# One load moved in the DMA queue, and the first two graphs' work put in another order, in a two-layer graph kernel

## The chip, the cores and the metric

The kernel runs on one core of a Trainium2 chip. A core has five engines that work side by side: TensorE (PE in the profile; PEld is its loading of weights), VectorE (DVE), ScalarE (ACT), GpSimd (POOL) and SyncE (SP), which here issues nearly all DMA transfers. The metric is the device time of one execution in microseconds (us); lower is better. Three runs of the kernel before took 2946.97 to 2951.11 us, with a median of 2949.02.

## The reference

64 graphs of N = 256 nodes with F = 512 features go through two layers; each adds its outcome to its input and normalises the rows. Layer 0 is a graph attention with 8 heads of 64 features: the logits are a sum of two numbers per node, and only neighbours are seen. Layer 1 is ordinary attention with the adjacency added to its weights.

```python
# layer 0
feats = einsum('bnf,hfu->bhnu', X, W)
e_self, e_neigh = feats . a_self, feats . a_neigh
att = softmax(leaky_relu(e_self[i] + e_neigh[j], 0.2) where A else -1e10)
x = layernorm(x + relu(att @ feats + b))
# layer 1
q, k, v = split(x @ W_qkv)
attn = softmax(q @ k.T / 8 where mask) * 0.33
attn = attn + 0.33 * adj + 0.33 * exp(-adj)          # both only where mask
x = layernorm(x + (attn @ v) @ W_out + b_out)
```

All numbers are 32-bit floats.

## The kernel before, in words

**Tiling.** A graph's 256 nodes are two tiles (T = 2) of 128 rows, its 512 features four chunks (C = 4) of 128. The four large products of a graph (features `pf`, queries and keys `pq`, values `pv`, output `po`) are each done with seven block products instead of eight (`seven`, `seven_rows`; steps "p1" to "p7"). For this, sums and differences of blocks are needed: of the activations (`left_factors`, giving `xC`, `hC`, `oC`) and, once, of the weights (`right_factors`, `combine_weights1`, giving parts of `wf_sb`, `wqk_sb`, `wv_sb`, `wo_sb`). PE multiplies and writes to PSUM; ACT copies the running sum of a chain of products to SBUF (L320), DVE adds the products that stand alone (L323).

**The order of the work** is written out by hand: `do(stage, b, step)` records the instructions of one step of graph b, and `in_order()` ties them to that order on each engine. So an engine runs its instructions in the order of the source, and one that waits holds up all behind it. Three routines follow one another:

- `start()` does layer 0 of graphs 0 and 1 and the q and k products of layer 1 of graph 0. Graph 0's and 1's features are plain products (`features`, L595) which DVE takes from PSUM (`copied`, L618, adding the bias). `maxima` transposes the logits to rows (`pr`), takes their maxima (L530) and broadcasts them with a small product (`pn`, L536); `columns` (L559, `nd`) and `factors` make the factors of the attention weights per column and per row, the latter spread over the partitions by products with a selection matrix (`pg`, L548) and kept in PSUM. `weights` multiplies them on DVE (`pT`, L669), `product` multiplies with the features on PE (`av`, L692). `shared` (L466 to L481) prepares the part of layer 1's weights that all heads share, `attention_vectors` (`pw`, `pwa`, L418) folds the attention vectors into the feature weights.
- A loop over b from 1 to 63 calls `attention0_beside_projections1(b)` and `attention1_beside_projections0(b)`. One turn holds work of four graphs: layer 1's attention of graph b−2 and b−1, layer 0's attention of b, its features of b+1. A turn of the trace is counted here from its first `pz` product (layer 1's scores).
- `end()` finishes the last graphs.

**The DMA queue.** SP issues the transfers of a turn in the order of the source. Around the change that is: `gs`, `gb` (row factors to DRAM and back, spread over the partitions), `rs`, `rb` (layer 1's inverse row sums, the same way, 1 MB), then `load_rows(b + 1)` (L138: x's rows, 0.5 MB, which `end` at L735 adds to layer 0's outcome), and in the next call `store` (`out_dram<-y`, L1113, 0.5 MB) and `rows_again` (`y<-hs`, L989, 0.5 MB: layer 0's outcome read back from DRAM). `rows_again` takes the buffer that `store` reads, so SP waits for that store to land before it issues it. `load_rows` takes the buffer of tag "hb".

Of the kernel before, what the change touches and what calls it, by code (L numbers as in the profile page):

```python
# [8 lines left out]
FT = mybir.dt.float32  # L9
# [8 lines left out]
def kernel(  # L18
# [56 lines left out]
    def ps_tile(shape, name):  # L75

        return psum.tile(shape, FT, tag="mm", name=name, bufs=4)

    matmul = nc.tensor.matmul
# [56 lines left out]
    def load_rows(b):  # L136
        X[b] = io.tile([P, T, F], FT, tag="hb", name=f"x_{b}", bufs=1)
        nc.sync.dma_start(X[b], x[b].rearrange("(t p) f -> p t f", p=P))  # L138
# [102 lines left out]
    def load_weights1():  # L241

        wk1 = work.tile([P, C2, F], FT, tag="p", name="wk1", bufs=5)
        wv12 = work.tile([P, C2, F2], FT, tag="both", name="wv12", bufs=4)
        parts = w_qkv.rearrange("(k c p) (h s u) -> s k c p h u", k=2, p=P, s=3, u=U)

        def get(dst, s, k, heads=slice(0, H)):
            for c in range(C2):
                nc.sync.dma_start(
                    dst[:, c].rearrange("p (h u) -> p h u", u=U), parts[s, k, c][:, heads]  # L250
                )

        get(wqk_sb[:, 0], 0, 0)
        get(wqk_sb[:, 1], 0, 1)
        get(wk1, 1, 0)
        get(wqk_sb[:, 6], 1, 1)
        get(wv_sb[:, 0], 2, 0, slice(0, HG))
        get(wv12, 2, 0, slice(HG, H))
        get(wv_sb[:, 1], 2, 1, slice(0, HG))
        get(wv_sb[:, 2], 2, 1, slice(HG, H))  # L260

        def combine(part):
            q1, q2, s1, s2, s3, s4, k2 = (wqk_sb[:, i] for i in range(7))
            if part == 0:
                nc.vector.tensor_add(s1, wk1, k2)
                nc.vector.tensor_sub(s2, s1, q1)
            elif part == 1:
                nc.vector.tensor_sub(s3, q1, wk1)
            elif part == 2:
                nc.vector.tensor_sub(s4, q2, s2)  # L270
            else:
                right_factors(wv_sb, wv12)
            in_order()

        return combine
# [163 lines left out]
    def proj0(b):  # L439
# [12 lines left out]
        FAR = {}  # L452
# [7 lines left out]
            nc.scalar.copy(mrow, MROW[b])  # L460
            FAR[1] = mrow

        def shared():
            mrow = FAR[1]
            CT[b] = work.tile([P, T, N], FT, tag="ct", name=f"ct_{b}", bufs=3)
            nc.vector.tensor_add(CT[b], pa, FAR[0])  # L466
            for j in range(T):
                nc.vector.scalar_tensor_tensor(
                    CT[b][:, j, :],
                    CT[b][:, j, :],  # L470
                    m33[:, j, b : b + 1],
                    mrow,
                    op0=ALU.mult,
                    op1=ALU.mult,
                )
# [43 lines left out]

        ROW = {}  # L520

        def maxima():

            ps = ps_tile([H, 2, N], f"pr_{b}")
            for s in range(2):
                for t in range(T):
                    transpose(ps[:, s, t * P : (t + 1) * P], V0[b][:, t, :, U + s])
            grow = small.tile([H, N + 1], FT, tag="grow", name=f"grow_{b}", bufs=1)
            nb = small.tile([H, 1], FT, tag="nb", name=f"nb_{b}", bufs=2)
            nc.vector.tensor_reduce(grow[:, N : N + 1], ps[:, 1, :], AX.X, ALU.max)  # L530
            nc.vector.tensor_scalar_mul(nb, grow[:, N : N + 1], -0.8)
            nc.scalar.activation(grow[:, :N], ps[:, 0, :], AF.Exp, bias=nb, scale=-0.8)
            diag = small.tile([H, H], FT, tag="diag", name=f"diag_{b}", bufs=1)
            nc.vector.tensor_scalar_mul(diag, ident[:H, :H], grow[:, N : N + 1])
            ROW["max"] = ps_tile([P, H], f"pn_{b}")
            matmul(ROW["max"], sel[:, H, :], diag, start=True, stop=True)  # L536
            ROW["rows"] = grow

        def factors():
            grow = ROW["rows"]  # L540
            nc.vector.tensor_scalar(
                grow[:, :N], grow[:, :N], 1.0, TINY, op0=ALU.min, op1=ALU.max
            )
            GB[b] = []
            for g in range(2):
                pg = psum.tile([P, HG, N], FT, tag="sc", name=f"pg_{b}_{g}", bufs=2)
                for k in range(HG):
                    matmul(  # L548
                        pg[:, k, :],
                        sel[:, g * HG + k, :],  # L550
                        grow[:, :N],
                        start=True,
                        stop=True,
                    )
                    GB[b].append(pg[:, k, :])

        def columns():
            nd = small.tile([P, T, H], FT, tag="nd", name=f"nd_{b}", bufs=2)
# [578 lines left out]
    def do(stage, b, step, *args):  # L1137

        if 0 <= b < NB:
            if (stage, b) not in S:  # L1140
                S[stage, b] = stages[stage](b)
            S[stage, b][step](*args)
            in_order()

    def start():
# [18 lines left out]
        attention_vectors(1, 0)  # L1164
        do("proj0", 0, "maxima")
        attention_vectors(0, 1)
        do("turned", 1, "xT")
        load(2)
        do("proj0", 0, "columns")
        do("proj0", 0, "factors")  # L1170
        for h in range(H):
            do("proj0", 0, "scaled", h)
            do("attend0", 0, "weights", h)
# [15 lines left out]
        attention_vectors(3, 1)  # L1189
        attention_vectors(2, 2)  # L1190
        attention_vectors(3, 2)
        combine_weights1(0)
        for t in range(T):
            for g in range(2):
                do("proj0", 1, "features", t, g)
        do("attend0", 0, "norm", tiles[0])
        do("proj0", 0, "shared")
        do("proj0", 1, "aT")
        load_rows(1)
        do("turned", 2, "xT")  # L1200
        right_factors(wf_sb, wf12)
        in_order()
        for t in range(T):
            for g in range(2):
                do("proj0", 1, "copied", t, g)
        do("proj0", 1, "maxima")
        do("proj0", 1, "columns")
        do("proj1", 0, "from_rows", 0)
        do("attend0", 0, "norm", tiles[1])
        do("proj1", 0, "qk", "p1")  # L1210
        do("proj1", 0, "from_rows", 1)
        do("proj1", 0, "blocks")
        do("proj1", 0, "hC")
        do("proj1", 0, "qk", "p2")
        do("proj0", 1, "far")
        do("proj0", 1, "factors")
        combine_weights1(1)
        combine_weights1(2)
        load_adj(2)
        do("proj1", 0, "qk_add", 11)  # L1220
        do("proj1", 0, "qk", "p6")
        for h in range(HG):
            do("proj0", 1, "scaled", h)
            do("attend0", 1, "weights", h)
        do("proj1", 0, "qk", "p5")
        do("proj1", 0, "qk", "p7")
        do("proj1", 0, "qk_add", 22)
        combine_weights1(3)
        for h in range(HG, H):
            do("proj0", 1, "scaled", h)  # L1230
            do("attend0", 1, "weights", h)
        do("proj1", 0, "qk", "p4")
        do("proj1", 0, "qk", "p3")
        do("proj1", 0, "qk_add", 12)
        do("turned", 2, "xC")

    def attention0_beside_projections1(b):


        if b > 1:  # L1240
            do("attend1", b - 4, "squares")
            do("proj1", b - 1, "qk", "p1")
            do("proj1", b - 1, "qk", "p2")
            do("proj0", b, "columns")
            do("attend1", b - 4, "store")
            do("attend1", b - 3, "rows_again")
            do("proj1", b - 1, "qk", "p6")
            for h in range(HG):
                do("proj0", b, "scaled", h)
                do("attend0", b, "weights", h)  # L1250
            do("proj1", b - 1, "qk_add", 11)
            for h in range(HG, H):
                do("proj0", b, "scaled", h)
            do("proj1", b - 1, "qk", "p5")
            for h in range(HG, H):
                do("attend0", b, "weights", h)
            do("proj1", b - 1, "qk", "p7")
            do("proj1", b - 1, "qk_add", 22)
            if b + 1 < NB:
                do("turned", b + 1, "xC")  # L1260
# [60 lines left out]
    def attention1_beside_projections0(b):  # L1321
# [32 lines left out]
        do("attend1", b - 2, "product", "p4")  # L1354
        do("proj0", b + 1, "bias")
        do("softmax1", b - 1, "inverted")
        if b + 1 < NB:
            load_rows(b + 1)
        do("attend1", b - 2, "product", "p3")
        do("attend1", b - 2, "product_add", 12)  # L1360
        if b == 1:
# [129 lines left out]
```

## Time and profile before

| | |
|---|---|
| runs, median (lowest to highest) | 2949.02 us (2946.97 to 2951.11) |
| profiled execution, its own time | 2945.5 us |
| its span, first to last instruction | 2943.7 us |
| PE busy | 2893.2 us, 98% |
| DVE busy | 2595.7 us, 88% |
| ACT busy | 1784.6 us, 61% |
| DMA, mean over the span | 123 GB/s |

The profile is one execution taken by the hardware profiler. "L12" is a line of the kernel. A row of the page's groups gives an engine's line and operation, output and input, the count, the busy time and the mean of one, and the engine's idle time just before with what ended it. The chain that ended last is followed back from the last instruction through whatever released each step; "issue" in it is time in which an engine waited for nothing that the profile shows. A row of the windows gives the stretch, then the busy time of PE, PEld, DVE, ACT and POOL in it, each with its count of instructions, and at its end the granted share of PE's clock, the busy share of the DMA engines and GB/s. The trace also holds a record of each DMA packet with its queue, start and size. Idle time of an engine that isn't the bottleneck costs nothing.

### The profile page before, as it was taken

To read this page: it belongs to the slowest core of one execution; us is meant where nothing else is said; L and a number is where in the kernel's file an instruction comes from. 1 tells how busy PE (TensorE), PEld (TensorE's weight loads), DVE (VectorE), ACT (ScalarE), POOL (GpSimd) and SP (SyncE) were. 2 spreads that over 40 slices of the span, in tenths; PEclk is the share of its full clock that TensorE was granted. 3 is DMA by queue.
4 is the path that set the end of the run, shared out by engine and by line. 5 is a ranking of instruction groups with operands and counts; after the bars stand their busy time and mean duration, and the time that the engine had idled before them with its cause. 6 is when DMAs were issued, how large, how long until landed. Compare 5 with 4: busy or idle time off the path is not lost.

```text
span 2943.7 us, 67840 instructions
## 1 busy us (share of the span) xinstructions
PE 2893.2 (98%) x26302; PEld 2475.2 (84%) x26302; DVE 2595.7 (88%) x5147; ACT 1784.6 (61%) x4905; POOL 210.1 (7%) x526
## 2 busy tenths in 40 slices
PE   8999999999999999999999999999999999999998
PEld 6788888888888888888888888888888888888886
DVE  5788989999989989999989989899998989989984
ACT  2556665666666666566666656666666666666563
POOL 0000000000000000000000000000000000000001
PEclk8999999999999999999999999999999999999999
DMA  6444454454454454454444554544544554545432
GB/s 127 94 125 117 128 137 109 131 136 116 127 138 109 130 130 122 128 127 125 130 120 124 138 117 127 136 108 130 140 110 127 135 119 129 124 120 139 117 109 69
DMA packets 778871, 362.23 MB, mean 123 GB/s; under 512 B 694604, under 2 KB 696636, under 8 KB 762552
## 3 DMA queue, kind: packets, MB, share of 16 engines
q1 hardware_dynamic: 776440, 357.37, 48.4%
q8 instruction: 210, 3.44, 0.5%
q14 instruction: 109, 0.89, 0.1%
q10 hardware_dynamic: 2112, 0.52, 0.1%
HBM read 289.42 MB, written 68.13 MB: 121 GB/s over the span
## 4 chain that ended last, share of the span: by engine, by line
PE 95%; DVE 2%; issue 1%; DMA 1%; ACT 1%; SPq 0%; POOL 0%; DVEq 0%; POOLq 0%; ACTq 0%
PE pq_p L311 27%; PE pf_p L311 13%; PE pv_p L311 13%; PE po_p L311 13%; PE av L692 9%; PE pz L859 8%; PE av L975 7%; PE pd L893 2%; PE pr L82 1%; PE po L1096 0%; PE pg L548 0%; SPq L114 0%; DMA gb<-gs 0%; DMA x<-in_x_dram 0%; ACT junk L363 0%
## 5 line engine op out<-in xcount | busy, mean ns | idle before, releaser
L311 PE MATMUL pq_p<-hC,wqk_sb 128*128 128x128 f32 x4096 | 495.2, 279 | 6.9 <-ACT qk L320 3.2
L311 PEld LDWEIGHTS pq_p<-hC,wqk_sb 128*128 128x128 f32 x4096 | 470.0, 193 | 24.4 <-ACT qk L320 17.3
L669 DVE SCALAR_TENSOR_TENSOR pT<-gb,ccol,at 128x256 f32<-128x256 f32 x992 | 403.1, 477 | 55.1 <-ACT ccol L566 55.1
L311 PE MATMUL pq_p<-hT,wqk_sb 128*128 128x128 f32 x3072 | 366.9, 276 | 2.0 <-DVE hT L121 1.4
L311 PEld LDWEIGHTS pq_p<-hT,wqk_sb 128*128 128x128 f32 x3072 | 360.9, 193 | 6.2 <-DVE hT L121 1.8
L873 ACT ACTIVATE p<-pz,hide 128x512 f32<-128x512 f32 x512 | 316.9, 686 | 76.5 <-PE pz L859 39.1
L965 DVE TENSOR_TENSOR p<-p,ct 128x1024 f32<-128x1024 f32 x252 | 308.7, 1225 | 8.6
L723 ACT ACTIVATE x<-av,rec 128x64 f32<-128x64 f32 x1008 | 221.0, 336 | 151.4 <-DVE rec L705 151.4
L958 DVE TENSOR_TENSOR p<-p,rb 128x1024 f32<-128x1024 f32 x252 | 304.1, 1207 | 4.9 <-DMA rb<-rs 4.9
L692 PE MATMUL av<-v,pT 128*64 128x65 f32 x8192 | 259.0, 224 | 13.7 <-issue 12.6
L692 PEld LDWEIGHTS av<-v,pT 128*64 128x64 f32 x8192 | 247.9, 139 | 24.1 <-issue 16.4
L859 PE MATMUL pz<-qk 64*128 64x256 f32 x2048 | 256.2, 389 | 0.9 <-ACT p L873 0.9
L626 ACT ACTIVATE v<-v 128x64 f32<-128x64 f32 x1024 | 251.8, 339 | 0.0
L311 PE MATMUL pf_p<-wf_sb,xC 128*128 128x264 f32 x992 | 251.2, 386 | 0.0
L311 PE MATMUL pv_p<-wv_sb,hC 128*128 128x256 f32 x1024 | 242.9, 380 | 4.1 <-ACT v L320 4.1
L859 PEld LDWEIGHTS pz<-qk 64*128 64x128 f32 x2048 | 187.1, 186 | 65.5 <-issue 46.0
L311 PE MATMUL po_p<-wo_sb,oC 128*128 128x256 f32 x992 | 234.5, 379 | 0.5 <-ACT o L320 0.5
L320 ACT COPY v<-pv_p 128x256 f32<-128x256 f32 x256 | 95.6, 373 | 225.8 <-PE pv_p L311 225.7
L975 PE MATMUL av<-p,v 128*64 128x256 f32 x2016 | 231.9, 382 | 0.2 <-DVE p L965 0.2
L311 PEld LDWEIGHTS pv_p<-wv_sb,hC 128*128 128x128 f32 x1024 | 194.9, 191 | 32.6 <-ACT v L320 4.9
L311 PEld LDWEIGHTS pf_p<-wf_sb,xC 128*128 128x128 f32 x992 | 187.8, 190 | 31.5 <-ACT v L320 0.3
L311 PEld LDWEIGHTS po_p<-wo_sb,oC 128*128 128x128 f32 x992 | 187.8, 190 | 27.2 <-ACT o L320 0.9
(163 smaller groups left out, 4442.1 us busy)
## 6 DMA issues: line engine op xcount, KB each, us to landing
rb<-rs SPq DMA_DIRECT2D x63, 1024.0 KB
gb<-gs SPq DMA_DIRECT2D x62, 1028.0 KB
hs<-x SPq DMA_DIRECT2D x64, 512.0 KB
xb<-in_x_dram SPq DMA_DIRECT2D x252, 128.0 KB
x<-in_x_dram SPq DMA_DIRECT2D x63, 512.0 KB
hb<-hs SPq DMA_DIRECT2D x252, 128.0 KB
y<-hs SPq DMA_DIRECT2D x63, 512.0 KB
out_dram<-y SPq DMA_DIRECT2D x63, 512.0 KB
```

What stands on the lines that cost most here:

```text
L311: matmul(d, lhsT, rhs, start=(p in FIRST and i == 0), stop=(i == len(todo) - 1), skip_group_check=True,)
L320: nc.scalar.copy(out[COPIES[p]], dst)
L626: nc.scalar.activation(V0[b][:, t, h, :U], V0[b][:, t, h, :U], AF.Copy, scale=V0[b][:, t, h, U : U + 1],)
L669: nc.vector.scalar_tensor_tensor(pT[h][:, j, :], GB[b][h], CCOL[b][:, j, h : h + 1], AT[b][:, j, :], op0=ALU.max, op1=ALU.mult,)
L692: matmul(av[r * half : (r + 1) * half, k, :], pT[h][:, j, i : i + half], V0[b][:, j, h, :UA], start=(j == 0), stop=(j == T - 1),)
L723: nc.scalar.activation(X1[b][:, t, h * U : (h + 1) * U], av[:, k, :U], AF.Copy, scale=REC0[g][:, t, k : k + 1],)
L859: matmul(pz[:, r, j, :], QK[b][rows, g, 1, j * P : (j + 1) * P], QK[b][rows, g, 0, :], start=True, stop=True,)
L873: nc.scalar.activation(p[:, :, j, :], pz[:, :, j, :], AF.Exp, bias=hide[:, j, b : b + 1], scale=U**-0.5,)
L893: matmul(pd[k * 32 : (k + 1) * 32, g // 2, :], ones, both[g][:, r, :], start=True, stop=True, tile_position=(0, 32 * k),)
L958: nc.vector.tensor_mul(p, p, REC[b][:, k : k + 2, g // 2, :] .unsqueeze(2) .to_broadcast([P, 2, T, N]),)
L965: nc.vector.tensor_add(p, p, CT[b].unsqueeze(1).to_broadcast([P, 2, T, N]))
L975: matmul(av[0][r * U : (r + 1) * U, g % 2, :], V1[b][:, j, 2 * g + r, :], PROBS[b][g][:, r, j, :], start=(j == 0), stop=(j == T - 1),)
```

## The change

In the loop, `load_rows` goes from the end of one call to the middle of the next: behind `rows_again` instead of behind `rb`. In `start()`, the order is changed and three steps are split: `combine_weights1(0)` in two halves (0 and 4), `shared` in two (0: the first addition; 1: the rest), `maxima` in two (the small product `pn` alone as part 1). For graph 0, `pn`, `columns` and `factors` come ahead of graph 1's transposes, and the first four heads' factors go to two PSUM tiles of two heads instead of one of four. For graph 1, its four feature products are copied by DVE one by one with other work between them; q's and k's first products of graph 0 follow behind them, and the transposes of graph 2 and the feature weights' `right_factors` go to the routine's end. No computation is added or left out, and PE, DVE, ACT and SP have the same instructions as before.

```diff
@@ combine(part)
             if part == 0:
                 nc.vector.tensor_add(s1, wk1, k2)
+            elif part == 4:
                 nc.vector.tensor_sub(s2, s1, q1)
@@ shared
-        def shared():
+        def shared(part=None):
             mrow = FAR[1]
-            CT[b] = work.tile([P, T, N], FT, tag="ct", name=f"ct_{b}", bufs=3)
-            nc.vector.tensor_add(CT[b], pa, FAR[0])
+            if part != 1:
+                CT[b] = work.tile([P, T, N], FT, tag="ct", name=f"ct_{b}", bufs=3)
+                nc.vector.tensor_add(CT[b], pa, FAR[0])
+            if part == 0:
+                return
@@ maxima
-        def maxima():
+        def maxima(part=None):
+            if part == 1:
+                ROW["max"] = ps_tile([P, H], f"pn_{b}")
+                matmul(ROW["max"], sel[:, H, :], ROW["diag"], start=True, stop=True)
+                return
...
-            ROW["max"] = ps_tile([P, H], f"pn_{b}")
-            matmul(ROW["max"], sel[:, H, :], diag, start=True, stop=True)
-            ROW["rows"] = grow
+            ROW.update(rows=grow, diag=diag)
@@ factors
-            for g in range(2):
-                pg = psum.tile([P, HG, N], FT, tag="sc", name=f"pg_{b}_{g}", bufs=2)
-                for k in range(HG):
...
+            h = 0
+            while h < H:
+                n = 2 if b == 0 and h < HG else HG
+                if n == 2:
+                    pg = ps_tile([P, n, N], f"pg_{b}_{h}")
+                else:
+                    pg = psum.tile([P, n, N], FT, tag="sc", name=f"pg_{b}_{h}", bufs=2)
+                for k in range(n):
+                    matmul(pg[:, k, :], sel[:, h + k, :], grow[:, :N], start=True, stop=True)
                     GB[b].append(pg[:, k, :])
+                h += n
@@ start
         attention_vectors(0, 1)
+        do("proj0", 0, "maxima", 1)
+        do("proj0", 0, "columns")
+        do("proj0", 0, "factors")
         do("turned", 1, "xT")
         load(2)
-        do("proj0", 0, "columns")
-        do("proj0", 0, "factors")
@@ start, behind attention_vectors(3, 2)
-        combine_weights1(0)
         for t in range(T):
             for g in range(2):
                 do("proj0", 1, "features", t, g)
         do("attend0", 0, "norm", tiles[0])
-        do("proj0", 0, "shared")
+        do("attend0", 0, "norm", tiles[1])
+        do("proj0", 1, "copied", 0, 0)
+        combine_weights1(0)
+        do("proj0", 1, "copied", 0, 1)
+        combine_weights1(4)
+        do("proj0", 1, "copied", 1, 0)
+        do("proj0", 0, "shared", 0)
         do("proj0", 1, "aT")
-        load_rows(1)
-        do("turned", 2, "xT")
-        right_factors(wf_sb, wf12)
-        in_order()
-        for t in range(T):
-            for g in range(2):
-                do("proj0", 1, "copied", t, g)
-        do("proj0", 1, "maxima")
-        do("proj0", 1, "columns")
+        do("proj0", 1, "copied", 1, 1)
         do("proj1", 0, "from_rows", 0)
-        do("attend0", 0, "norm", tiles[1])
-        do("proj1", 0, "qk", "p1")
         do("proj1", 0, "from_rows", 1)
         do("proj1", 0, "blocks")
+        load_rows(1)
+        do("proj0", 1, "maxima")
+        do("proj1", 0, "qk", "p1")
+        do("proj0", 1, "maxima", 1)
+        do("proj0", 1, "columns")
+        do("proj1", 0, "qk", "p2")
         do("proj1", 0, "hC")
-        do("proj1", 0, "qk", "p2")
+        do("proj0", 1, "factors")
+        do("proj0", 0, "shared", 1)
         do("proj0", 1, "far")
-        do("proj0", 1, "factors")
-        combine_weights1(1)
-        combine_weights1(2)
         load_adj(2)
         do("proj1", 0, "qk_add", 11)
+        combine_weights1(1)
         do("proj1", 0, "qk", "p6")
         for h in range(HG):
             do("proj0", 1, "scaled", h)
             do("attend0", 1, "weights", h)
+        combine_weights1(2)
         do("proj1", 0, "qk", "p5")
         do("proj1", 0, "qk", "p7")
-        do("proj1", 0, "qk_add", 22)
-        combine_weights1(3)
         for h in range(HG, H):
             do("proj0", 1, "scaled", h)
+        do("proj1", 0, "qk_add", 22)
+        for h in range(HG, H):
             do("attend0", 1, "weights", h)
         do("proj1", 0, "qk", "p4")
         do("proj1", 0, "qk", "p3")
         do("proj1", 0, "qk_add", 12)
+        combine_weights1(3)
+        do("turned", 2, "xT")
         do("turned", 2, "xC")
+        right_factors(wf_sb, wf12)
+        in_order()
@@ attention0_beside_projections1(b), b > 1
             do("attend1", b - 4, "store")
             do("attend1", b - 3, "rows_again")
+            load_rows(b)
@@ attention1_beside_projections0(b)
         do("softmax1", b - 1, "inverted")
-        if b + 1 < NB:
-            load_rows(b + 1)
```

More of the change, by code (lines that the diff above doesn't have):

```diff
@@ L544, in factors @@
             GB[b] = []
-            for g in range(2):
-                pg = psum.tile([P, HG, N], FT, tag="sc", name=f"pg_{b}_{g}", bufs=2)
-                for k in range(HG):
[L548 to L554, printed above, removed]
+            h = 0
[7 more added lines that the diff above has]
+                    matmul(pg[:, k, :], sel[:, h + k, :], grow[:, :N], start=True, stop=True)
                     GB[b].append(pg[:, k, :])
+                h += n
         def columns():
```

## The prediction

> **What bounds the kernel now.** I read the busy table and the chain that ended last first: TensorE (PE) carries 95% of it, so only time in which PE stands still or runs at half clock can be won or lost.
>
> ```profile
> PE 2893.2 (98%) x26302; PEld 2475.2 (84%) x26302; DVE 2595.7 (88%) x5147; ACT 1784.6 (61%) x4905; POOL 210.1 (7%) x526
> PE 95%; DVE 2%; issue 1%; DMA 1%; ACT 1%; SPq 0%; POOL 0%; DVEq 0%; POOLq 0%; ACTq 0%
> ```
>
> Then the same chain in order of time, two turns of the loop (columns: start, us, what):
>
> ```profile
> 828.74 5.62 PE pq_p L311 x48
> 834.37 3.88 PE av L692 x128
> 838.25 3.77 PE pq_p L311 x32
> ...
> 873.13 5.62 PE pq_p L311 x48
> 878.75 3.88 PE av L692 x127
> 882.63 1.34 issue
> 883.97 0.27 PE av L692
> 884.24 3.77 PE pq_p L311 x32
> ...
> 919.12 5.62 PE pq_p L311 x48
> ```
>
> One turn takes 44.39 us, the next 45.99: PE stood 1.34 us near the end of `av` and waited for nothing shown ("issue"). PE's waits list eleven such stops, 9 on `av` (12.6 us) and 2 on the `pq_p` behind it (2.0 us); their turns exceed 44.39 by 1.4, 1.8, 1.6, 1.3, 1.2, 1.5, 1.7, 2.2, 1.1, 1.5 and 4.0, together 19.2 us. The page's DMA part names a suspect, and the DMA queue's timeline says what runs then:
>
> ```profile
> q8 instruction: 210, 3.44, 0.5%
> ...
> 873.62 0.32 SPq L939 DMA_DIRECT2D rb<-rs  x1
> 873.99 0.43 SPq L138 DMA_DIRECT2D x<-in_x_dram  x1
> 875.74 0.39 SPq L1113 DMA_DIRECT2D out_dram<-y  x1
> 882.19 0.36 SPq L989 DMA_DIRECT2D y<-hs  x1
> ```
>
> 3.44 MB is about 64 bytes for each of PE's 52,604 loads and matmuls: queue 8 fetches PE's instructions, in 16 KB blocks of 256. The stops lie at every 256th PE instruction, counted in the trace. By its packet records the fetch began at 881.65, when `rb`, `x` and `out` had just drained, and PE went on 2.32 us later; in all eleven stops that is 2.2 to 2.5.
>
> At the start of the program the windows show idle PE and, behind it, half clock (0.50 in the third row):
>
> ```profile
> 35.00:49.00 14.00, 13.97 (x155) 12.35 (x152) 10.44 (x27) 3.51 (x7) 3.85 (x8) 1.00 0.45 85
> 49.00:52.50 3.50, 0.02 (x1) 0.03 (x1) 3.47 (x8) 0.00 (x0) 0.00 (x0) 0.94 0.00 0
> 52.50:62.30 9.80, 8.01 (x34) 6.72 (x35) 1.47 (x6) 3.23 (x8) 0.00 (x0) 0.50 0.32 79
> ...
> 51.66 1.44 DVE L618 TENSOR_TENSOR v<-pf,b_bc 128x264 f32<-128x264 f32 x4
> ...
> 52.48 0.38 PE L82 MATMUL pr<-ident,v 128*8 128x128 f32 x1 [3.50 <-DVE v L618]
> ```
>
> [...] fetches due in this burst mostly start at +27.0 to +27.6 after the turn's first `pz`, as it ends. [...] the trace's slow stretches last 3.41, 10.24 or 13.65 us.
>
> **The loop.** Times are from the turn's first `pz` (turn at 809.84). Before: `rb` packets +20.0 to +23.3, `x` and `out` together to +27.5, none until `y` from +29.0 to +31.2. `x` now goes behind `y`; no bytes change. `out` alone has 16 packets of 2 KB per engine at 84 ns, 1.35 us, and about 1 us to get up to rate: the burst ends near +25.7. `y` is issued when `out` has landed (now +28.04 in the middle, then +26.3), its packets begin near +27.1, so a gap of 1.3 us stays in which a fetch gets in. A fetch from +25.6 is there at +27.9; the blocks ran out at +27.6 to +28.1. Each stop falls from 1.1 to 2.4 us to about 0.2. The longest also cost 1.7 us by half clock over 3.41 us. Sum: 19.2 − 11 × 0.2 = −17.0.
>
> Nothing on SP is delayed by `x`'s wait but `xb`, which doesn't issue before +38. `x` itself is due at L735, +33.92; issued near +26.7 behind `y`'s 0.5 MB, its packets end near +31 and land by +31.6: 2.3 us spare, so the move costs nothing. `out` and `y` only come sooner.
>
> **The start.** (a) Graph 0: `pg` began at 24.11, behind `nd` (held by a 1.23 us transpose) and eight `pwa` products at half clock. Now `pwa` goes right behind `pr` at 20.25 and takes 1.05 (its time at 35.05), then `pn` 0.3, `nd` 0.1, the clamp of the row factors (L541) 0.3: `pg` at 22.25. Its split into 2, 2 and 4 heads lets DVE start early, but PE's own 7.19 us of `pg` and the `av` behind them set the end: −1.9.
> (b) Graph 1: DVE did 9.2 us of other work (42.47 to 51.66) before the four feature copies, 1.44. They now stand between its pieces, and only 3.85 us of the work (L265, L266, L466, one transpose) remain there. `pf` ends at 47.1, and PE goes on at full clock with two `ph` 1.1 each, `pr` 0.9, p1 1.9, `pn` 0.3, p2 2.0 to 54.3; the clamp is done by 54.4; `pg` 3.7 to 58.2, before 67.9: −9.7. Products p6 to p3 took 11.8 (67.83 to 79.59), half a window at half clock among it, and end at 69.9.
> (c) What moved ends elsewhere. DVE from 52.3: hC 1.7, clamp 0.3, rest of shared 1.9, qk_add 0.7, L268 1.2, pT 3.2, L270 1.2, to 62.5; it waits for p7's copy (75.72 − 67.83 behind p6's start) to 66.1; qk_add 0.7, pT 3.2, qk_add 0.7, to 70.7. Then four `wv` sums 2.65, the transpose of graph 2 1.2, xC 1.6 and four `wf` sums 2.75 stand ahead of `rec`: 78.9, before 84.07: −5.1. Before, the transpose and the `wf` sums sat in the 9.2 us and the `wv` sums in a DVE idle of 5.6 us at 70 to 75; that cover is gone.
> (d) The ACT copy of the value product waits on `rec` and 3.4 us of L723, so PE now idles some 6.9 us (76.1 to 83.0) instead of 1.81, and one slow window of 3.41 us behind it costs 1.7. At the first `pz` (98.80) the gain is 5.1 less at most 1.7; I take −4. Bounds: −8 if the clock stays up at 21 to 35 and 76 to 86, −1 with two more slow windows. On SP, graph 1's `x` now waits behind the `hs` store for ACT's normalisation (about 45 instead of 42.3), and graph 2's adjacency behind it; their readers come after 70. `load(2)` waits for a transpose 1.3 us later, but SP reaches it only at 35.97.
>
> Sum: −17 − 4 = −21 us on the profiled execution, 2945.5 (span 2943.7), hence 2924.5. The median of the runs shown is 3.5 higher, 2949.0, so **2928.0**.
>
> **Rivals.** (1) Only part of the stops goes: `out` lands sooner than estimated and `y` with `x` behind it, now 4 us of burst, shuts out fetches of blocks entered at +25.0 to +25.7, harmless today. For it: fetches wait for whole bursts. Against: blocks entered from +26 on have 9 us to run. Half the gain, 8 us, goes: 2936. (2) The fetch isn't freed (its lateness comes from `rb` and `out`): the start alone counts, 2945, no measurable change. Against: the delayed starts follow the end of `x` and `out`, not of `rb`. (3) Slower: `x` lands late. It decides from about +35, 1 us behind L735's present start, as PE's value products wait for DVE then; at 0.6 us a turn over 61 turns, 37 − 21: 2965. For it: `y` was once issued at +31.1; against: the 2.3 us. (4) A better start, with the clock up: 2924.
>
> **How the numbers follow.** Both parts as worked out 0.63 (own range 2922 to 2936), rival 1 0.15, rival 2 0.10, rival 3 0.07, rival 4 0.05. Two of ten may lie outside: 2920 to 2943. About 0.2% (5.9 us) is what a measurement here can tell from no change: faster 0.83 (all but rivals 2 and 3), same 0.10, slower 0.07.
>
> **What would show it.** "Issue" ahead of `av` under 3 us in total, and turns of 44.39 nearly throughout; `x` issued behind `y`; the instruction packet at +25.6. First `pz` near 95; no gap at 49 to 52; PE idle before the third value product grown to some 7 us. Wrong: stops as many as before but elsewhere, or DVE idle before L735 on a DMA.

## The result and the profile after

| | before | changed |
|---|---|---|
| runs, median (lowest to highest) | 2948.53 us (2946.97 to 2951.11) | 2919.55 us (2917.97 to 2920.05) |
| profiled execution, its own time | 2945.5 us | 2917.97 us |
| its span | 2943.7 us | 2916.2 us |
| first `pz`, the end of `start()` | 98.80 us | 90.32 us |
| turns over 44.39 us, their excess together | 19.9 us | 1.05 us |

The kernel became faster: the ratio is 0.990, with a 95% interval of 0.9883 to 0.9917. The forecast of 2928.0 was 8.45 us too high, and the measured time lies 0.45 us below the forecast range. The span fell by 27.5 us: 8.5 ahead of the first `pz`, 19.0 between it and the first `pz` of the turn that leads into `end()`, and nothing in the last 120.0 us.

The busy table, the instruction queue and the chain that ended last, from the page of the changed kernel:

```profile
PE 2882.9 (99%) x26302; PEld 2468.0 (85%) x26302; DVE 2594.9 (89%) x5147; ACT 1784.9 (61%) x4905; POOL 210.5 (7%) x526
...
q8 instruction: 210, 3.44, 0.5%
...
PE 96%; DVE 1%; DMA 1%; ACT 1%; issue 0%; SPq 0%; POOL 0%; ACTq 0%; DVEq 0%; POOLq 0%
```

PE has the same 26302 products and is busy for 10.3 us less as well: 5.7 of them ahead of the first `pz`, where fewer products ran at half clock, and 4.5 in the loop (counted in the two traces). "Issue" has gone from the chain, while queue 8 fetches as many instruction blocks as before: 210 packets of 16,384 bytes in either trace, where PE has 53,880 instructions before and 53,893 after, semaphores and drains among them, 210.5 times 256. The loop, in the same chain in order of time (start, us, what), at the two turns that answer to those shown of before:

```profile
816.95 5.62 PE pq_p L312 x48
822.58 3.88 PE av L699 x128
826.46 3.77 PE pq_p L312 x32
...
866.97 3.65 PE av L699 x120
870.61 0.19 issue
870.80 0.45 PE av L699 x7
871.26 3.77 PE pq_p L312 x32
```

The second turn still crosses a block of instructions in `av`, but for 0.19 us instead of 1.34. It is the only stop of the kind that PE's waits still list; the two rows of PE's waits also show what has grown in `start()`, a wait of 6.7 us for ACT's copy of the value product:

```profile
PE pv_p L312 <- ACT v L321: 9.8, 4, 6.7
...
PE av L699 <- issue: 0.2, 1, 0.2
```

The DMA queue's timeline in the first of those turns (its `pz` at 798.05) has `x` at the end:

```profile
817.45 0.31 SPq L946 DMA_DIRECT2D rb<-rs  x1
819.57 0.39 SPq L1120 DMA_DIRECT2D out_dram<-y  x1
823.50 0.37 SPq L996 DMA_DIRECT2D y<-hs  x1
823.92 0.46 SPq L138 DMA_DIRECT2D x<-in_x_dram  x1
```

`y` is issued at +25.45 here and at +25.83 in the middle of all turns (before +28.03), `x` at +26.25. The packet records say the same from the other side. Counted at each half us after a turn's first `pz` are the packets of the data queue in flight, as a mean over 56 turns, and behind the stroke the instruction fetches that start in the half us that follows (worked out from the packet records; the third kernel is that of the experiment "x between out and y"):

```
              before       changed      x between out and y
 +23.0      15.3 / 1     15.7 / 0     15.8 / 0
 +24.0      12.4 / 0     16.8 / 1     16.5 / 0
 +24.5      13.7 / 0     15.6 / 4     17.0 / 4
 +25.0      13.9 / 1      6.6 / 3     16.1 / 2
 +25.5      16.6 / 0      1.8 / 15    16.4 / 0
 +26.0      16.8 / 0      0.4 / 8     16.4 / 20
 +26.5      16.7 / 5      0.3 / 2      5.8 / 9
 +27.0      13.5 / 25     4.9 / 1      6.8 / 5
 +27.5       4.5 / 21    10.1 / 4     10.6 / 3
```

With some 16 packets in flight hardly a fetch starts; most start in the half us in which the burst empties. The changed kernel empties it at about +25.0, 2.3 us sooner than before.

In `start()`, PE's timeline of the changed kernel (start, us, instructions, and the idle before them in brackets):

```profile
21.57 5.28 PE L560 MATMUL pg<-grow,sel 8*128 8x256 f32 x16 [0.46 <-DVE grow L547]
...
44.20 1.04 PE L82 MATMUL ph<-ident,x 128*128 128x128 f32 x8
...
49.77 3.72 PE L560 MATMUL pg<-grow,sel 8*128 8x256 f32 x16
53.41 7.25 PE L312 MATMUL pq_p<-hC,wqk_sb 128*128 128x128 f32 x48
...
77.64 4.79 PE L312 MATMUL pv_p<-wv_sb,hC 128*128 128x256 f32 x12 [6.65 <-ACT v L321]
...
90.32 2.00 PE L866 MATMUL pz<-qk 64*128 64x256 f32 x16
```

The wait for graph 1's feature copies is gone, and graph 1's `pg` ends at 53.5 (before 67.9). The first row is the one to remember: the same 16 products as in the third take 5.28 us there and 3.72 here.

### The profile page after: what moved, and what is told of

Its sections match the earlier page's. It is cut to its first block, busy times and chain, and to the rows that moved or that the text cites. A ratio compares the mean times of both kernels' runs of the same rounds, so it can differ in the third digit from the quotient of the medians.

```text
span 2916.2 us, 67798 instructions
## 1 busy us (share of the span) xinstructions
PE 2882.9 (99%) x26302; PEld 2468.0 (85%) x26302; DVE 2594.9 (89%) x5147; ACT 1784.9 (61%) x4905; POOL 210.5 (7%) x526
## 4 chain that ended last, share of the span: by engine, by line
PE 96%; DVE 1%; DMA 1%; ACT 1%; issue 0%; SPq 0%; POOL 0%; ACTq 0%; DVEq 0%; POOLq 0%
PE pq_p L312 28%; PE pf_p L312 13%; PE pv_p L312 13%; PE po_p L312 13%; PE av L699 9%; PE pz L866 8%; PE av L982 8%; PE pd L900 2%; PE pr L82 1%; PE po L1103 0%; PE pg L560 0%; PE pf L602 0%; DMA wf_sb<-in_L_gnn_W_dram 0%; DMA gb<-gs 0%; ACT junk L364 0%
## 5 line engine op out<-in xcount | busy, mean ns | idle before, releaser
L312 PEld LDWEIGHTS pq_p<-hC,wqk_sb 128*128 128x128 f32 x4096 | 468.7, 192 | 21.7 <-ACT qk L321 17.1
L312 PEld LDWEIGHTS pv_p<-wv_sb,hC 128*128 128x128 f32 x1024 | 196.0, 192 | 37.9 <-ACT v L321 9.7
L982 PEld LDWEIGHTS av<-p,v 128*64 128x64 f32 x2016 | 139.0, 137 | 85.0 <-issue 20.9
```

Of the source, the lines that this page charges most:

```text
L312: matmul(d, lhsT, rhs, start=(p in FIRST and i == 0), stop=(i == len(todo) - 1), skip_group_check=True,)
L982: matmul(av[0][r * U : (r + 1) * U, g % 2, :], V1[b][:, j, 2 * g + r, :], PROBS[b][g][:, r, j, :], start=(j == 0), stop=(j == T - 1),)
```

## The experiments

Theory: the loop's gain comes from PE's instruction fetches, which a burst of data packets holds up until it has drained; the start's gain comes from the order of the work, and its size depends on PE's clock. Rivals: the stops belong to the work at which they appear; `x` must stand behind `y`; the start's share is nothing; DVE's tail rather than PE's clock sets the start's end.

The kernel before was measured beside each group of experiments: 2945.11 us for the first four, 2944.77 for the next four, 2945.93 for the last three. The changed kernel, measured again in the second group, took 2919.99. In the table, "excess" is what the turns take over 44.39 us, and "half clock" is how long PE's clock stood at 0.50 between 10 us and the first `pz`, from windows of 0.5 us.

| kernel | median us | ratio to before (95%) | excess | first pz | half clock |
|---|---|---|---|---|---|
| before (profile shown) | 2948.53 | | 19.9 | 98.80 | 27.3 |
| changed (profile shown) | 2919.55 | 0.990 (0.9883 to 0.9917) | 1.05 | 90.32 | 17.1 |
| changed, again | 2919.99 | 0.9914 (0.9899 to 0.9929) | 1.9 | 93.29 | 23.9 |
| the load alone | 2926.39 | 0.9939 (0.9925 to 0.9954) | 1.4 | 95.68 | 20.5 |
| the start alone | 2935.08 | 0.997 (0.9958 to 0.9981) | 14.4 | 92.27 | 20.5 |
| x between out and y | 2924.82 | 0.9935 (0.992 to 0.9949) | 4.7 | 92.07 | 20.5 |
| x ahead of rs | 2920.59 | 0.9921 (0.9906 to 0.9936) | 1.8 | 94.63 | 27.3 |
| blocks shifted (one time) | 2951.69 | | 21.1 | 102.20 | 30.7 |
| graph 0 in the old order | 2922.46 | 0.9922 (0.9907 to 0.9937) | 1.6 | 94.63 | 23.9 |
| no split of the factors | 2920.14 | 0.9909 (0.9892 to 0.9925) | 1.2 | 95.08 | 27.3 |
| sums into DVE's idle | 2913.26 | 0.989 (0.9873 to 0.9906) | 2.2 | 87.10 | 17.1 |
| pg over 128 rows | 2915.54 | 0.9894 (0.988 to 0.9909) | 2.4 | 86.47 | 6.8 |
| both of these | 2908.07 | 0.9869 (0.9855 to 0.9884) | 1.6 | 80.39 | 3.4 |

**The load alone**, in the kernel before:

```diff
             do("attend1", b - 3, "rows_again")
+            load_rows(b)
...
         do("softmax1", b - 1, "inverted")
-        if b + 1 < NB:
-            load_rows(b + 1)
```

> The kernel before, with load_rows moved behind rows_again in the loop and nothing else. Burst theory (an instruction fetch waits until the burst of rb, x and out has drained; without x the burst ends 2 us sooner): the turns become 44.39 us throughout, PE's issue waits before av fall from 12.6 us to under 1, the first pz stays near 98.8; 19 us less, about 2929 to 2930. Rival (the stops vanish because the new start shifts the instruction blocks): the stops stay, 2947 to 2949. Rival (x lands late at L735): DVE waits on the DMA there, turns over 44.5.

Measured: 18.7 us faster than before, with the excess down to 1.4. The first `pz` didn't stay near 98.8: it came at 95.68, although this kernel's `start()` is that of before. It stood at half clock for 20.5 us in this profile and for 27.3 in that of before. One profile of each kernel therefore doesn't measure what a new `start()` is worth.

**The start alone** is the changed kernel with that edit undone:

> The changed kernel with load_rows back behind rb: the new start alone. Burst theory: the first pz near 90.3 as in the changed kernel, some ten stops of 1 to 2.4 us before av remain in the loop (15 to 20 us in all); about 2937 to 2941. Rival (the start's shift of the blocks removed the stops): no stops, 2919 to 2921.

Measured: 10.0 us faster than before, and the stops are back. PE's waits in it:

```profile
PE av L699 <- issue: 9.6, 7, 1.6
...
PE pq_p L312 <- issue: 2.0, 2, 1.1
```

18.7 and 10.0 make 28.7; the whole change gave 29.0 against 2948.53, but 25.1 against the 2945.11 beside which the two parts were measured. They don't simply add, because the new `start()` changes the stops too: it has 13 more semaphore instructions on PE (33 instead of 20 ahead of the first `pz`, counted in the traces), so that the blocks of 256 end elsewhere in the turns. The start alone has nine stops and an excess of 14.4 us, the kernel before eleven and 19.9. That there are stops is due to where `load_rows` stands; how many there are depends on `start()` as well. The loop is worth 15.1 to 18.7 us (2935.08 − 2919.99, 2945.11 − 2926.39), the start 6.4 to 10.0 (2926.39 − 2919.99, 2945.11 − 2935.08). Some 5.5 of these 10.0 are the difference of the two excesses, which leaves 4.5 to 6.4 us for `start()` itself (an estimate).

**x between out and y**, in the changed kernel:

```diff
             do("attend1", b - 4, "store")
+            load_rows(b)
             do("attend1", b - 3, "rows_again")
-            load_rows(b)
```

> The changed kernel with load_rows between store and rows_again: x is issued later than before, but joins the burst of rb and out ahead of the pause in which SP waits for out to land. Burst theory: the burst again ends 2 us later, near +27.5, so the stops are back at ten or so turns; 2936 to 2941. Rival (any place behind out will do, since out then lands sooner and y comes sooner): no stops, 2918 to 2922.

PE's waits in it:

```profile
PE av L699 <- issue: 2.1, 4, 0.7
...
PE pq_p L312 <- issue: 1.0, 1, 1.0
```

The same 2 MB of `rb`, `out` and `x` lie in one burst, as before the change, and yet most of the gain stays. The table of packets shows why the stops are few: this burst empties near +26.2, not +27.3. With `x` ahead of `out` only 12 to 14 packets were in flight from +24 to +25; with `x` behind `out` it is 16 throughout. The fetches still wait for the burst to empty: 20 start within +26.0 to +26.5, in which the number in flight falls from 16.4 to 5.8. My error was to take the burst's end from its bytes; the order of its transfers moves it too. Why the engines aren't full when `x` follows `rb` directly stays open.

**x ahead of rs**, in the changed kernel, so that `x` is issued at about +12, before the burst:

```diff
         do("proj1", b, "hT")
+        if b + 1 < NB:
+            load_rows(b + 1)
...
             do("attend1", b - 3, "rows_again")
-            load_rows(b)
```

> The changed kernel with load_rows ahead of rs and rb, behind the transposes that free its buffer (hT): x follows gb at about +14 to +19, and the burst from +20 holds rb and out alone. Burst theory: stops gone, as fetches delayed by gb and x have 8 us or more to the next block; 2918 to 2922. Rival (x must be behind y): stops as before, 2936 to 2941.

Measured 2920.59, with an excess of 1.8: the same as the changed kernel. So what matters is that `x` is out of the burst between `rb` and `out`; the place behind `y` isn't needed.

**Blocks shifted**, in the kernel before:

```diff
             pwa = WA[g, "logits"] = ps_tile([P, C, 4], f"pwa_{g}")
-            for c in range(C):
+            for c in [c for c in range(C) for _ in range(5 if g == 3 else 1)]:
```

> The kernel before with 16 products more in start(): each of the four pwa products of g = 3 is done five times into the same PSUM cells, the outcome unchanged. That puts 16 loads and 16 matmuls, 32 PE instructions, ahead of the loop, and moves every boundary of a 256-instruction block by 32 instructions against the work. If the stops belong to the block boundaries, they stay at multiples of 256 of PE's instruction count, the number is again between 8 and 14 (15 to 22 us), and most of the turns that have one are other turns than before (or the stop lies 32 instructions sooner in its turn). If they belong to the work itself (a semaphore or a buffer that the trace does not show), the same turns have them at the same product.

PE's waits in it:

```profile
PE av L692 <- issue: 11.5, 8, 1.9
...
PE pq_p L311 <- issue: 2.6, 4, 1.0
```

Twelve stops again, at the same remainder (194) of PE's instruction count modulo 256 as in the kernel before; the count takes in PE's semaphore instructions. Counted from 0, the turns that had one before were 2, 6, 17, 21, 25, 32, 36, 40, 47, 51 and 55; now they are 1, 5, 12, 16, 20, 24, 31, 35, 39, 46, 50 and 54. Each of the eleven is one turn earlier, and one is new. A stop that belonged to the work or to a buffer would not move to another turn because of 32 instructions put in ahead of the loop.

**Graph 0 in the old order** (changed kernel; factors in two tiles of four heads):

```diff
         do("proj0", 0, "maxima")
-        attention_vectors(0, 1)
         do("proj0", 0, "maxima", 1)
-        do("proj0", 0, "columns")
-        do("proj0", 0, "factors")
+        attention_vectors(0, 1)
         do("turned", 1, "xT")
         load(2)
+        do("proj0", 0, "columns")
+        do("proj0", 0, "factors")
```

> The changed kernel with graph 0's part of start() back in the old order: pn behind pr, then pwa, graph 1's transposes and loads, and only then columns and factors, in two tiles of four heads. The loop is that of the changed kernel. Prediction's step (a) says 1.9 us later. If instead the earlier pg also shortens the half-clock stretch, as the two traces suggest (5.28 against 7.19 us for the same products), the cost is 2 to 5 us: first pz at 92 to 95 and 2922 to 2925. If the order of graph 0 does not matter, 2920 and pg at 5.3 us.

Measured 2922.46 against 2919.99: 2.5 us, where step (a) had 1.9; the runs don't tell these two apart. `pg` starts at 24.48 in this kernel's profile, 2.6 us later than in the changed kernel beside it (21.84). Both stood at half clock for 23.9 us, so that an earlier `pg` shortens that time isn't shown.

**No split of the factors**, in the changed kernel:

```diff
-                n = 2 if b == 0 and h < HG else HG
+                n = HG
```

> The changed kernel with the factors of graph 0 in two PSUM tiles of four heads instead of two, two and four. The prediction gave the split nothing, because PE's own pg products and the av behind them set the end: 2919 to 2921, first av within 0.3 us. If the split matters, DVE's first weights wait for four heads instead of two and av comes 1 us or more later: 2921 to 2923.

Measured 2920.14: no difference that these runs can tell. In its profile `pg` took 7.19 us, all of it at half clock, as in the kernel before. So it did in "x ahead of rs", which has the split, and the first `av` started at 29.48 here and at 29.30 there.

**Sums into DVE's idle**, in the changed kernel:

```diff
             do("proj0", 1, "scaled", h)
+        combine_weights1(3)
+        do("turned", 2, "xT")
         do("proj1", 0, "qk_add", 22)
...
         do("proj1", 0, "qk_add", 12)
-        combine_weights1(3)
-        do("turned", 2, "xT")
-        do("turned", 2, "xC")
-        right_factors(wf_sb, wf12)
-        in_order()
...
         do("proj1", b - 1, "v_add", 11)
+        if b == 1:
+            do("turned", 2, "xC")
+            right_factors(wf_sb, wf12)
+            in_order()
```

> The changed kernel with DVE's tail of start() taken from in front of rec: the four wv sums and the transpose of graph 2 go into DVE's 3.9 us idle ahead of qk_add 22, and graph 2's xC and the wf sums go behind v_add 11 of the next routine. If these 8.2 us in front of rec are what makes PE wait 6.65 us for the ACT copy of the value product and sets its clock to half behind it, the wait falls below 1 us, no half clock follows, the first pz comes at 82 to 85 and the time falls by 5 to 9 us to 2911 to 2915. If ACT's own chain (L723 and the copies) sets that wait, PE still idles over 4 us there and the time stays within 2 us of the changed kernel's. If the moved sums only come late for their new readers, DVE or PE waits in the first turn for as much as is won and the time is that of the changed kernel.

PE's timeline in it, the row that answers to the one with 6.65 us of idle:

```profile
75.28 2.86 PE L312 MATMUL pv_p<-wv_sb,hC 128*128 128x256 f32 x12 [0.43 <-ACT v L321]
```

6.7 us faster than the changed kernel, and the first `pz` at 87.10 instead of 93.29. The wait falls to 0.43 us and the products behind it take 2.86 us instead of 4.31 in the changed kernel measured beside it (4.79 in the first profile). So DVE's sums in front of `rec` caused both. The first `pz` was expected at 82 to 85; this kernel still stood at half clock for 17.1 us ahead of it, and the moved sums make PE wait twice, 0.21 us for `wf_sb` and 0.35 for `v`.

**pg over 128 rows**, in the changed kernel; the added rows are zeros, the products as many and as long:

```diff
-    sel = work.tile([H, H + 1, P], FT, tag="rb", name="sel", bufs=1)
+    sel = work.tile([P, H + 1, P], FT, tag="rb", name="sel", bufs=1)
...
-        sel[:, :H, :], ident[:H, :H].unsqueeze(2).to_broadcast([H, H, P])
+        sel[:, :H, :], ident[:, :H].unsqueeze(2).to_broadcast([P, H, P])
...
-            grow = small.tile([H, N + 1], FT, tag="grow", name=f"grow_{b}", bufs=1)
+            full = small.tile([P, N + 1], FT, tag="grow", name=f"grow_{b}", bufs=1)
+            nc.gpsimd.memset(full, 0.0)
+            grow = full[:H]
...
-                    matmul(pg[:, k, :], sel[:, h + k, :], grow[:, :N], start=True, stop=True)
+                    matmul(pg[:, k, :], sel[:, h + k, :], ROW["full"][:, :N], start=True, stop=True)
```

> The changed kernel with the pg products of both graphs done over 128 rows instead of 8: the selection matrix and the row factors get 120 rows of zeros (one POOL memset per graph), count and columns of the products are the same, and so is the outcome. Theory: [...] products over 8 rows count as next to nothing; then the half clock behind graph 1's pg (3.4 us near 54 to 58) goes, the stretch behind graph 0's pg (6.8 to 16 us from 23) shrinks to at most one window of 3.41 us, pg takes 3.7 to 4.5 us instead of 5.3 to 6.5, the first pz comes at 84 to 89 and the time falls by 3 to 7 us to 2913 to 2917. Rival: only standing still counts (PE idles 1.0, 1.0 and 0.5 us at 17.5 to 21.5); then the same stretches stay, and the time is within 1.5 us of the changed kernel's 2920.

The windows of the changed kernel, measured again (the clock is the third number from the end):

```profile
24.50:28.00 3.50, 3.50 (x9) 2.37 (x8) 2.07 (x6) 1.43 (x6) 0.00 (x0) 0.50 0.84 165
28.00:31.50 3.50, 3.50 (x61) 3.29 (x62) 3.18 (x9) 0.00 (x0) 0.00 (x0) 0.50 1.14 229
31.50:35.00 3.50, 3.50 (x30) 3.36 (x28) 0.95 (x7) 0.00 (x0) 0.00 (x0) 0.50 1.32 194
```

The same windows of the kernel with 128 rows, and the two `pg` of its PE timeline:

```profile
24.50:28.00 3.50, 3.50 (x71) 2.95 (x71) 3.50 (x10) 1.59 (x7) 0.00 (x0) 1.00 1.04 178
28.00:31.50 3.50, 3.50 (x81) 3.42 (x83) 2.48 (x11) 0.58 (x1) 0.00 (x0) 1.00 0.97 214
31.50:35.00 3.50, 3.50 (x49) 3.30 (x45) 2.88 (x9) 1.40 (x3) 0.66 (x2) 1.00 0.62 138
```

```profile
22.10 3.69 PE L562 MATMUL pg<-grow,sel 128*128 128x256 f32 x16 [0.55 <-DVE grow L549]
...
47.39 3.69 PE L562 MATMUL pg<-grow,sel 128*128 128x256 f32 x16
```

In all six windows PE is busy for the whole 3.50 us by its row, so standing still can't be what keeps the clock at half there. How the first stretch begins is another matter: PE's short waits at some 17 to 22 (0.24, 1.04 and 0.46 us in the changed kernel's first profile) lie ahead of it in every kernel, and with 128 rows it still began once ("both of these", below). With 128 rows there is no half clock at all until PE's idle of 6.64 us behind the value products; the first `pz` comes at 86.47 instead of 93.29, and the time is 4.4 us less than 2919.99. That idle and its 6.8 us of half clock remain, as they should. Differences from one execution to another alone don't explain it: in the eleven profiles with 8 rows (before, and ten of the experiments' and the changed kernel's) the stretch that covers graph 0's `pg` lasted 6.8 to 20.5 us, in the two with 128 rows none and 3.4.

Graph 1's `pg`, ahead of which PE doesn't wait for long, shows it more clearly. The stretches of the clock's records in `start()`, full and half, are multiples of 3.413 us long in the traces (3.413 to 23.89 in the changed kernel's first). Worked out from the traces in steps of that length: in nine of the eleven profiles products over 8 rows filled 0.64 to 1.00 of one step, with PE busy all through it, and the next step was at half clock. In the other two they filled at most 0.62 of a step ("the load alone"; and the changed kernel again, where they lay across two steps, with 0.56 and 0.53), and the clock stayed up. With 128 rows they filled 1.00 and 0.91 of a step, and it stayed up too. So what was changed, the rows, makes the difference here; with 8 rows, whether the clock fell went with the share of one step that these products filled, 0.64 or more against 0.62 or less.

Few rows aren't the only cause, though. The second and third window of the first table hold next to no `pg`, but `av`, `pw` and `pwa`, and the clock stays at half. And in "blocks shifted" 48 `pwa` products of 128 rows and 4 columns, one behind another from 42.58 to 48.78 us, went with half clock from 47.2 to 54.1.

**Both of these** together:

> The kernel of e8 (DVE's sums taken from in front of rec) with the pg products over 128 rows as well. If both causes are what they were said to be, their gains add: 2907 to 2911, and the first pz at 78 to 83. If the half clock behind pg is not due to the 8 rows, 2913 as e8.

Measured 2908.07, 11.9 us less than the changed kernel's 2919.99; alone they gave 6.7 and 4.4. (The changed kernel without the split, measured beside this one, took 2920.14.) It is the fastest of all, 37.9 us below the kernel before measured beside it. Ahead of the first `pz` half clock is left once, for 3.4 us at 21.5 to 25.5, behind PE's short waits at 17 to 21.5.

**The changed kernel again:**

> The changed kernel once more, on the chip of the other runs of this call, as their measure. Within 2917 to 2922 us. It also shows how much start() differs from one execution to another: first pz at 90.3 in the profile shown; if the clock falls in other stretches, up to 3 us more or less, with the turns unchanged at 44.39.

Its first half-clock stretch lasted 17.1 us (22.5 to 40) where the first profile had 6.8 (23.5 to 30.5), its first `pz` came 3.0 us later, and its median differs by 0.4 us.

## Why the prediction was wrong, and what in it was right

**Bound and mechanism: right.** PE carries the chain, and time was won only where PE stood still or ran at half clock: by the busy tables PE is busy for 10.3 us less with the same products, and idle for 17.2 us less. Of the cases foreseen it was the likeliest that happened, with both parts, and it brought more than was worked out for it: 29.0 us where 21 were forecast. Three terms of the sum were off: the start, the stops left in the loop, and the 3.5 us added for the median.

**The loop, −17.0 predicted, −19.0 in the profiles.** The stops belong to blocks of 256 instructions (shown by "blocks shifted") and come from where `x` was loaded (shown by "the load alone" and "the start alone"). Mis-sized was above all the last term, 0.2 us left for each of eleven stops, 2.2 us: the changed turns exceed 44.39 by 1.05 us in all, of which 0.19 is a stop on a block. Another 0.7 us is that 19.9 us stood over 44.39 when all turns are counted, not 19.2; together 1.85 of the 2.0. The step behind the small stops is "the burst ends near +25.7": it is nearly empty at +25.5 already (1.8 packets in flight), so fetches start from +25.0 (15 of them in the half us from +25.5). At before's stops PE went on 2.2 to 2.5 us after the fetch began; on that measure these are there at about +27.3 to +28.3 (an estimate), just as the blocks at hand run out (+27.6 to +28.1). `y`'s place was predicted at +26.3 and measured at +25.83; `x` at +26.7, measured at +26.25.

**`x`'s slack: right, but with little to spare at times.** DVE waited for `x` once in the whole run, 0.3 us, by its waits, and the reader still started at +33.93 in the middle. So rival 3 didn't happen.

**The start, −4 predicted, −8.5 and −5.5 in the two profiles: the step that failed.** It failed at (a), "PE's own 7.19 us of `pg` and the `av` behind them set the end". 7.19 us is the time of these products at half clock; I took it as theirs. They took 5.28 us in the first profile, 6.45 in the second, and 3.69 with the clock up. The bound of −8 ("if the clock stays up at 21 to 35") named this, but the chosen value carried the old clock over. That bound was too small as well: 8.5 us were gained although the clock did fall in both stretches (23.6 to 30.4, 74.8 to 81.6). Down the first profile the difference runs like this: `pf` ended at 44.4 instead of 47.1 (0.7 from an earlier `pg`, 1.9 from a shorter one). In (b), two `ph` of 1.1 each were read off a row that ran at half clock. The groups of PE's instructions up to 98 us, each shape apart (count, busy time and mean of one in ns, idle before), before:

```profile
L548 PE MATMUL pg<-grow,sel 8*128 8x256 f32 x32 | 10.9, 510 | 0.3 <-DVE grow L541 0.3
...
L82 PE MATMUL ph<-ident,x 128*128 128x128 f32 x8 | 2.2, 428 | 0.0
```

and changed:

```profile
L560 PE MATMUL pg<-grow,sel 8*128 8x256 f32 x32 | 9.0, 438 | 0.5 <-DVE grow L547 0.5
...
L82 PE MATMUL ph<-ident,x 128*128 128x128 f32 x8 | 1.0, 272 | 0.0
```

The two `ph` took 1.04 us together, so that PE went from the end of `pf` to graph 1's `pg` in 5.4 us instead of 7.2. Products p6 to p3 took the 11.8 us that were predicted and ended at 65.2 instead of 69.9. Hence in (c) `rec` came at 73.70, not 78.9 (77.15 in the second profile, whose clock fell for longer). DVE's order ahead of it was as worked out: in the changed kernel DVE does the `wv` sums, the transpose, xC and the `wf` sums without a gap from 65.83 to 73.70. (d) was right: an idle of 6.65 us where 6.9 were forecast; the half clock behind it lasted 6.8 us, not 3.41, but the products in it were few, and their 12 took 4.79 us instead of 2.86, 1.9 us where 1.7 were taken.

**The median.** The prediction added 3.5 us, by which before's median lay above its profiled execution; after, it is 1.6. So the 8.45 us between forecast and result are 4.5 of the start, 2.0 of the loop and 1.9 of this offset. With the second profile of the changed kernel the 8.0 us from 2928.0 to its 2919.99 divide otherwise: 1.5 of the start, 1.2 of the loop, 1.5 of the last 48 us and 3.9 of the offset. In the later groups the kernel before had medians of 2944.77 to 2945.93, so there the 3.5 us above its profiled 2945.5 weren't found again.

How much the start's term was too small is thus known only as 1.5 to 4.5 us, and that the first profile shows the larger value is in part luck. At the same half clock the new start is 3.4 to 4.2 us ahead of the old (20.5 us: 92.27 and 92.07 against 95.68; 27.3 us: 94.63 against 98.80). The rest comes from less half clock, which changes from one execution to the next in both. On average the new start has less of it: the granted clock that each run lists has a mean of 0.9940 in four runs of "the load alone" and 0.9954 in eight of the changed kernel, some 8 us of half clock less (an estimate, since each figure is rounded to 0.001).

**The rivals.** Rival 1 (half the gain, `out` sooner and `y` with `x` behind it shutting out other fetches) didn't happen: fetches do start later in that second burst, 10 and 12 of them at +29.5 and +30.0, but no turn pays for it. Rival 2 fell with "the load alone". Rival 4, a better start with the clock up, came partly true beside the loop's full gain.

Where the clock's steps lie against the work differs between executions of one and the same kernel: graph 1's `pg` filled 0.77 of one step in the changed kernel's first profile, and 0.56 and 0.53 of two in its second. Half clock ahead of the first `pz` lasted 17.1 us in the first and 23.9 in the second.

## What to carry to other kernels

A busy row isn't a duration until the clock beside it has been read (the same 16 `pg` took 7.19 us at half clock before, and 3.72 at full clock after): take each duration that goes into a sum from a stretch at full clock, and put the clock's own cost in a separate term with its own bounds. Read the clock in more than one execution, too, of the old kernel as of the new: what it did at this kernel's start differed from one to the next (17.1 and 23.9 us of half clock). If an engine stops with nothing to wait for, count its instructions modulo 256 (all eleven stops before had the remainder 194) and look for what its fetch queues behind; moving a load of 0.5 MB out of the burst, to either side, was worth more (15.1 to 18.7 us) than the whole reordering of the start (6.4 to 10.0). Before work is moved to the end of a routine to get it out of the way, ask which wait of the bottleneck engine stands there: the cheap place was DVE's idle of 3.9 us in front of `qk_add`.

## What the hardware showed that I had not expected

- Products over 8 rows didn't hold PE's clock up, even back to back: behind graph 1's `pg` (in the changed kernel's first profile 49.77 to 53.5, PE without a gap) it fell to half in nine of eleven profiles, those in which these products filled 0.64 or more of one 3.413 us step. With 120 rows of zeros added it fell behind neither `pg`, and nothing took longer (3.69 against 3.72 us). Zeros in the operands were enough. Products of 128 rows but 4 columns didn't hold it up either (48 of them in "blocks shifted", with half clock from 47.2 on, while they ran). Other numbers of rows and columns weren't tried, and what exactly the clock counts stays open.
- The half-clock stretches have lengths of 3.41, 6.83, 10.2, 13.7, 17.1 and 20.5 us, multiples of one step. In kernels with the same `start()`, 6.8 us more of it went with a first `pz` 3.0 us (changed) or 3.1 us (before) later.
- An instruction fetch hardly ever started while some 16 data packets were in flight, though it has a queue of its own (queue 8): in the 56 turns before, 0, 0 and 5 started in the three half us from +25.5, with 16.6 to 16.8 packets in flight, and 25 and 21 in the next two, as these fell from 13.5 to 4.5. With 12 to 14 in flight it went both ways: 0, 0 and 1 fetches in the three half us from +24.0 in the kernel before, 4 and 3 in the two from +28.0 in the changed kernel. The same bytes in another order (`out` ahead of `x`) drained about 1 us sooner (near +26.2 against +27.3), and two thirds of the stops' time went with that alone (excess 4.7 us against 14.4 with `x` ahead of `out` and the same start).
